# The first two attention tiles' values computed beside the last chunk of the first layer

## The chip, the cores and the metric

The kernel runs on one core of a Trainium2 chip. The metric is the device time of one execution in microseconds (us), shown as the median of several runs; lower is better. Beside these runs there is one profiled execution, from which every duration in this text is taken.

## The reference, cut to what matters

The input x is (4, 384, 64, 64) in float32, in other words 4 images of 384 channels and 4096 tokens. Two layers follow each other, each with a group norm ahead and a residual around it.

```python
x = x + L0(_gn(x), ...)   # a Mamba block over the 4096 tokens of each image
x = x + L1(_gn(x), ...)   # outlook attention, 3x3 windows at stride 2, 12 heads

# L0, after in_proj, causal convolution and silu:
def step(h, inp):
    dt_t, B_t, C_t, x_t = inp
    dA = jnp.exp(dt_t[:, :, None] * A[None])
    dBx = (dt_t * x_t)[:, :, None] * B_t[:, None, :]
    h = dA * h + dBx
    return h, jnp.einsum('bdn,bn->bd', h, C_t)
y = (jnp.moveaxis(ys, 0, 1) + xc * D) * _silu(z)
out = jnp.einsum('bld,cd->blc', y, out_proj_w)

# L1:
pooled = x.reshape(B, C, h, S, w, S).mean(axis=(3, 5))
a = softmax((einsum('bchw,ac->bhwa', pooled, attn_w) + attn_b) * scale)  # 9x9 a head and pixel
v = jnp.einsum('blkc,koc->blko', patches, Wg)       # nine 384x384 matrices
o = jnp.einsum('bnlpq,bnlqd->bnlpd', a, v)          # then folded back (3x3, overlapping)
y = jnp.einsum('bchw,oc->bhwo', folded, proj_w) + proj_b
```

The group norm needs the statistics of a whole image, so the second layer can start on an image only when the first layer has ended with that image. Image 0 is ready long before image 3 ends the first layer.

## The kernel before, in words

**The first layer** (`mamba_layer`, line 80) cuts the 4 images into 68 chunks of 241 tokens. Of a chunk, a *front* (norm, input projection, convolution, `dt`) runs ahead, then twelve *units* are scanned (768 channels of 16 states; a unit is two scans), then an *end* projects the result (`e_project`, line 681) and stores it to `x1` in device memory (`e_store`, line 689). A loop over steps `s` (line 776) writes the order of all engines out by hand. In step `s` unit `s` is scanned (DVE, `s_scan`), unit `s+1` gets its inputs (DVE, `s_inputs2`) and decays (ACT, `s_decay`), POOL multiplies unit `s-1` by C (`s_outputs`, line 642) and prepares unit `s+2` (`s_inputs`, line 598), PE sums the pair up to unit `s-2` into `y` each second step (`s_sum`, line 647), DVE gates a pair by `y` a step later (`s_gate`), and SP fetches units four steps ahead (`s_fetch`, line 585). Every engine executes its instructions in the order written: the class `InOrder` (line 34) puts all of them in program order, and since it issues them, the profile has them all under its line 45 and tells them apart by the names of the tiles.

The 68 chunks make 816 units. At `front_end`, step 803, the last front is done, the fronts' pools are closed (`fronts.close()`), and from there on each step ends with one call of `behind` (line 823), which is where work of the second layer is handed in. Matmul results of fronts and ends go through the PSUM pool `pmm`, two buffers in turn.

In the kernel before, `behind` steps through `outlook_weights` (line 1103), which loads the weights of the second layer: `wa` (attention weights, three DMAs), `wv` (the nine value matrices, three DMAs), then `ab`, `wpr`, `pb` and `own`, one DMA a step.

**The second layer** (`outlook_layer`, line 827) cuts the 4 images into 32 tiles of 8 rows, each 128 output pixels. A tile goes through these functions:

- `p_load` (887): 9 rows of `x1` to `xr` by DMA
- `p_pixels` (898): six ACT instructions apply the norm and sort the pixels into `xp` by window column; POOL clears the border; three DVE adds make the pooled pixels `t2`
- `p_weights` (932): 12 matmul records `psa`, then a chain on DVE and ACT to the softmax `at`, stored to `ads` in device memory
- `p_values` (957): for each of nine window positions three matmuls (six records) `psv`, an ACT copy to `vst`, and a DMA of three positions to `vds` in device memory
- `p_fetch_weights`, `p_fetch_values` (979, 982): both come back from device memory in another arrangement (`ain`, `vin`)
- `p_blocks` (985): block-diagonal weights `bd`, on ACT for rows 0 and 2, on POOL for rows 1 and 3
- `p_attend`, `p_fold` (1002, 1018): attention of one of four row pairs on PE into one PSUM buffer `ps`, added into `fold` by DVE
- `p_project` (1034): output projection `pso`, residual, store

The loop at line 1072 works on three tiles at once: `new` (i+2) is loaded and gets its pixels, `mid` (i+1) its weights and values, `old` (i) is attended. It begins at i = -2, when only tile 0 as `new` exists. `ads` and `vds` have two buffers each, with nine rows of zeros at their ends, written once at the start of the layer.

Of the kernel before, what the change touches and what calls it, by code (L numbers as in the profile page):

```python
# [12 lines left out]
P = 128  # L13
# [66 lines left out]
def mamba_layer(ctx, tc, x, w, x1, sc1, bi1, consts, behind):  # L80
# [695 lines left out]
    for s in range(-4, NU * (len(chunks) + 2)):  # L776
        k, m = divmod(s, NU)
        if m % 2 == 0 and unit(s + 4) is not None:
            s_fetch(s + 4)
        parts(s, EARLY)  # L780
        if m % 4 == 3 or s >= NU * len(chunks):
            norm_part(False)

        if (u := unit(s + 1)) is not None:
            s_inputs2(u)
        if (u := unit(s - 3)) is not None and not u.first:
            s_gate(u)
        parts(s, READY)

        b, ci = chunks[k][:2] if 0 <= k < len(chunks) else (B, 0)  # L790
        if b + 1 < B:
            n, e = divmod(NU * ci + m - 3, NU // 2)
            if e == 0 and 0 < n <= NCB * NX:
                x_stat(b + 1, n - 1, pending.pop())
            if e == 1 and 0 <= n < NCB * NX:
                pending.append(x_load(b + 1, n))
            if e == 2 and n == NCB * NX:
                x_coeffs(b + 1)
        for i in range(2):
            if (u := unit(s)) is not None:  # L800
                s_scan(u, i)
            if i == 1:
                parts(s, SCAN)
            if (u := unit(s + 1)) is not None:
                if i == 0:
                    s_carry(u)
                s_decay(u, i)
            if i == 0 and (u := unit(s - 1)) is not None:
                s_save(u)
        if (u := unit(s - 1)) is not None:  # L810
            s_outputs(u)
        norm_part(True)
        parts(s, POOL)
        if (u := unit(s + 2)) is not None:
            s_inputs(u)
        if (u := unit(s - 2)) is not None and not u.first:
            s_sum(unit(s - 3), u)
        parts(s, MID)
        parts(s, LATE)
        if s == front_end:  # L820
            fronts.close()
        if s >= front_end:
            behind()


@with_exitstack
def outlook_layer(ctx, tc, x1, w, out, sc1, bi1, consts, weights):

    nc = tc.nc
    B, _, H, W = out.shape
    NR = 4
    NW = W // 2
    NT = H // (2 * NR)
    ROWS = 2 * NR + 1  # L840
    HO = HEADS * KK
    NA = HO * KK
    NH = NA // 2
    NGW = 3
    VQ = 3
    scale = float(HD) ** -0.5
    pe, ve, ae, gp, sp = (
        InOrder(tc, e) for e in (nc.tensor, nc.vector, nc.scalar, nc.gpsimd, nc.sync)
    )

    wp = ctx.enter_context(tc.tile_pool(name="zero1", bufs=1))
    wa, ab, wv, wpr, pb, own = (weights[name] for name in ("wa", "ab", "wv", "wpr", "pb", "own"))

    ve.tensor_scalar_mul(wa, wa, 0.25)
    io = ctx.enter_context(tc.tile_pool(name="io1", bufs=3))
    act = ctx.enter_context(tc.tile_pool(name="act1", bufs=2))
    dram = ctx.enter_context(tc.tile_pool(name="dscr1", bufs=1, space=bass.MemoryType.DRAM))
    pa = ctx.enter_context(tc.tile_pool(name="pa", bufs=1, space=bass.MemoryType.PSUM))
    pv = ctx.enter_context(tc.tile_pool(name="pv", bufs=3, space=bass.MemoryType.PSUM))
    pt = ctx.enter_context(tc.tile_pool(name="pt", bufs=1, space=bass.MemoryType.PSUM))  # L860


    zero = wp.tile([KK, C], F32, tag="zero", name="zero")
    ve.memset(zero, 0.0)
    vds, ads = [], []
    for i in range(2):
        vd = dram.tile([P * KK + KK, C], F32, tag=f"vd{i}", name=f"vd{i}")
        ad = dram.tile([P * KK + KK, HO], F32, tag=f"ad{i}", name=f"ad{i}")
        sp.dma_start(vd[P * KK :, :], zero)
        sp.dma_start(ad[P * KK :, :], zero[:, :HO])  # L870
        vds.append(vd)
        ads.append(ad)

    class Tile:
        pass

    tiles = []
    for i in range(B * NT):
        c = Tile()
        c.i = i  # L880
        c.b, c.t = divmod(i, NT)
        c.first, c.last = c.t == 0, c.t == NT - 1
        c.lo = 1 if c.first else 0
        c.vin, c.ain, c.bd = {}, {}, {}
        tiles.append(c)

    def p_load(c):

        c.xr = io.tile([P, NCB, ROWS, W], F32, tag="xr", name="xr")
        for cb in range(NCB):  # L890
            sp.dma_start(
                c.xr[:, cb, c.lo :, :],
                x1[c.b, :, (2 * NR * c.t + c.lo - 1) * W : (2 * NR * c.t + ROWS - 1) * W].rearrange(
                    "(p cb) (r w) -> p cb r w", cb=NCB, w=W
                )[:, cb],
            )

    def p_pixels(c):


        b = c.b
        xp = act.tile([P, 3, NCB, ROWS, NW], F32, tag="xp", name="xp")
        gp.memset(xp[:, 0, :, :, 0:1], 0.0)
        if c.first:
            gp.memset(xp[:, :, :, 0, :], 0.0)
        for kj in range(3):
            j0 = 1 if kj == 0 else 0
            w0 = 2 * j0 + kj - 1
            for odd in range(2):
                r0 = 1 if odd else 2 * c.lo  # L910
                i0 = NR + 1 if odd else c.lo
                i1 = ROWS if odd else NR + 1
                ae.activation(
                    xp[:, kj, :, i0:i1, j0:],
                    c.xr[:, :, r0:ROWS:2, w0 : W - 2 + kj : 2],
                    AF.Identity,
                    bias=bi1[:, b : b + 1],
                    scale=sc1[:, b : b + 1],
                )
        c.xf = xp.rearrange("p kj cb r w -> p kj cb (r w)")  # L920
        c.t2 = act.tile([P, NCB, NR * NW], F32, tag="t2", name="t2")
        t3 = act.tile([P, NCB, NR * NW], F32, tag="t3", name="t3", bufs=1)
        ve.tensor_add(c.t2, pixel(c, 4), pixel(c, 5))
        ve.tensor_add(t3, pixel(c, 7), pixel(c, 8))
        ve.tensor_add(c.t2, c.t2, t3)

    def pixel(c, q):
        ki, kj = divmod(q, 3)
        row = (0, NR + 1, 1)[ki]
        return c.xf[:, kj, :, row * NW : (row + NR) * NW]  # L930

    def p_weights(c):

# [23 lines left out]
    def p_values(c, q):  # L957

        if q % VQ == 0:
            c.vst = act.tile([P, VQ, C], F32, tag="vst", name="vst", bufs=3)  # L960
        pix = pixel(c, q)
        psv = pv.tile([P, 512], F32, tag="pv", name="psv")
        for cb in range(NCB):
            pe.matmul(psv[:, :C], pix[:, cb, :], wv[:, cb, q, :], start=(cb == 0), stop=(cb == NCB - 1))
        ae.copy(c.vst[:, q % VQ, :], psv[:, :C])
        if q % VQ == VQ - 1:
            sp.dma_start(
# [101 lines left out]

        return (old, r) if r < NR else (mid, r - NR)  # L1070

    for i in range(-2, len(tiles) + 1):
        new, mid, old = tile_at(i + 2), tile_at(i + 1), tile_at(i)
        for r in range(NR):
            if old and r == 0:
                p_fetch_values(old, 0)
            if old and r + 1 < NR:
                p_fetch_values(old, r + 1)
            if mid and r == 0:
                p_weights(mid)  # L1080
            c, k = ahead(old, mid, r + 2)
            if c:
# [3 lines left out]
            for n, q in enumerate(qs):  # L1086
                if c:
                    p_blocks(c, k, n, len(qs))
                if mid:
                    p_values(mid, q)  # L1090
            if r == 0:
                if done := tile_at(i - 1):
                    p_project(done)
                if new:
                    p_load(new)
            if old:
                p_attend(old, r)
                p_fold(old, r)
            if r == 2 and new:
                p_pixels(new)  # L1100


def outlook_weights(ctx, tc, w, weights):

    wp = ctx.enter_context(tc.tile_pool(name="wp1", bufs=1, side="right"))
    sp = InOrder(tc, tc.nc.sync)
    na = HEADS * KK * KK
    shapes = {
        "wa": [P, NCB, na],
        "ab": [P, na],  # L1110
        "wv": [P, NCB, KK, C],
        "wpr": [P, NCB, NCB, P],
        "pb": [P, NCB],
        "own": [GW * KK, GW],
    }
    for name, shape in shapes.items():
        weights[name] = wp.tile(shape, F32, tag=name, name=name)
    for name in ("wa", "wv"):
        for cb in range(NCB):
            sp.dma_start(weights[name][:, cb], w[name][:, cb])  # L1120
            yield
    for name in ("ab", "wpr", "pb", "own"):
        sp.dma_start(weights[name], w[name])
        yield


@with_exitstack
def layers(ctx, tc, w, out):
# [14 lines left out]
    sc1 = cp.tile([P, B], F32, tag="sc1", name="sc1")  # L1143
    bi1 = cp.tile([P, B], F32, tag="bi1", name="bi1")
    consts = (blk12, ident, eps, one)
    weights = {}
    later = outlook_weights(ctx, tc, w, weights)
    mamba_layer(
        tc, x.rearrange("b c h w -> b c (h w)"), w, x1, sc1, bi1, consts, lambda: next(later, None)
    )  # L1150
    for _ in later:
        pass
    outlook_layer(tc, x1, w, out, sc1, bi1, consts, weights)


def layouts(inputs):
# [63 lines left out]
```

## Time and profile before

| | us |
|---|---|
| time, median of 3 runs (6319.99 to 6328.01) | 6324.49 |
| time of the profiled execution | 6322.35 |
| span of its trace, first to last instruction | 6320.6 |
| busy in it: PE / DVE / ACT / POOL | 5612.9 / 5377.6 / 4986.4 / 5311.3 |
| first fetch of a second-layer weight (`wa`, on SP) | at 4963.25 |
| last product on POOL in the first layer | ends 5037.64 |
| norm of the last image, last matmul | ends 5056.28 |
| `psa` of tiles 0, 1 and 2 | start 5070.77, 5104.21, 5140.01 |

The profile has busy times of the engines, their course in 40 slices of the span (158 us each), windows of any length, groups of instructions, and timelines for one engine: start, length, engine, operation, written tile <- read tiles, how many are merged in the line, and in brackets the idle time ahead and who ended it. PE is the matmul engine, PEld its weight loads, DVE the vector engine, ACT the scalar engine, POOL GpSimd, SP the engine that issues the DMAs.

### The profile page before, as it was taken

How to read it: one execution, taken by the hardware profiler on the slowest of the kernel's cores; microseconds unless marked ns; L12 is line 12 of the kernel's file. 1: busy time of each engine (PE TensorE's matmuls, PEld its weight loads, DVE VectorE, ACT ScalarE, POOL GpSimd, SP SyncE). 2: the span in 40 equal slices, each digit the busy share in tenths (PEclk: the TensorE clock that was granted, in tenths of full speed). 3: DMA queues.
4: the chain of work that ended last, by engine and by line, in shares of the span. 5: the costliest groups of instructions: out<-in, count | busy, mean ns of one | idle time of the engine just before them, and what ended most of it. 6: DMA issues, size and time to landing. Idle time of an engine off the chain costs nothing. (4 is left out here: it accounts for less than half of the span.)

```text
span 6320.6 us, 113305 instructions
## 1 busy us (share of the span) xinstructions
PE 5612.9 (89%) x40488; PEld 3956.3 (63%) x40488; DVE 5377.6 (85%) x4785; ACT 4986.4 (79%) x11842; POOL 5311.3 (84%) x2046
## 2 busy tenths in 40 slices
PE   6888888898888888888888888988898689999999
PEld 5666666666666666666666666666666345555555
DVE  4999999999999999999999999999999844554444
ACT  3888898888998889888898888889888644444453
POOL 3999999999999999999999999999999824333333
PEclk9899999999999999999998999999999799999999
DMA  4556555555555555555555555545555444445544
GB/s 127 132 134 149 147 131 140 126 139 147 134 142 139 139 139 134 131 142 137 147 145 131 135 128 138 139 127 135 130 133 138 137 138 164 166 165 171 170 165 143
DMA packets 635514, 893.42 MB, mean 141 GB/s; under 512 B 129913, under 2 KB 529067, under 8 KB 634436
## 3 DMA queue, kind: packets, MB, share of 16 engines
q1 hardware_dynamic: 634948, 886.17, 52.2%
q8 instruction: 319, 5.23, 0.4%
q14 instruction: 247, 2.02, 0.1%
HBM read 660.11 MB, written 225.70 MB: 140 GB/s over the span
## 5 line engine op out<-in xcount | busy, mean ns | idle before, releaser
L45 DVE TENSOR_TENSOR_SCAN h<-da,h 128x968 f32<-128x968 f32 x1632 | 3449.0, 2154 | 76.5 <-issue 51.8
L45 ACT ACTIVATE da<-dtr,aneg 128x241 f32<-128x241 f32 x6528 | 3036.6, 465 | 303.1 <-DVE h L45 137.8
L45 POOL TENSOR_TENSOR h<-h,bc 128x1928 f32<-128x1928 f32 x816 | 3228.9, 3957 | 12.8 <-DVE h L45 10.6
L45 POOL TENSOR_TENSOR h<-dxr,bc 128x964 f32<-128x964 f32 x816 | 1626.2, 1993 | 106.6 <-PE y L45 88.6
L45 PE MATMUL ps_in<-u,win 128*128 128x241 f32 x4896 | 1081.5, 374 | 85.8 <-DVE dtx L45 78.0
L45 PEld LDWEIGHTS ps_in<-u,win 128*128 128x128 f32 x4896 | 913.0, 191 | 252.1 <-DVE dtx L45 102.4
L45 POOL TENSOR_TENSOR bd<-ain,own 99x1188 f32<-99x1188 f32 x192 | 413.1, 2180 | 772.4 <-DMA ain<-ad 608.4
L45 DVE TENSOR_TENSOR h<-dxr,bp 128x964 f32<-128x964 f32 x816 | 928.1, 1137 | 105.2 <-PE y L45 88.9
L45 PE MATMUL y<-h,ssum 128*32 128x241 f32 x13056 | 909.0, 406 | 36.6 <-POOL h L45 35.4
L45 PEld LDWEIGHTS y<-h,ssum 128*32 128x32 f32 x13056 | 433.5, 119 | 455.0 <-issue 210.9
L45 PE MATMUL ps_cv<-xb,cdiag 128*128 128x241 f32 x3264 | 694.3, 368 | 6.0 <-ACT neg L45 4.5
L45 PEld LDWEIGHTS ps_cv<-xb,cdiag 128*128 128x128 f32 x3264 | 611.0, 189 | 79.3 <-issue 13.5
L45 PE MATMUL psv<-wv,xp 128*128 128x384 f32 x1728 | 587.9, 492 | 0.8 <-ACT vst L45 0.8
L45 PE MATMUL ps_xd<-xc,wx 128*56 128x241 f32 x816 | 300.5, 548 | 322.0 <-ACT xc L45 322.0
L45 ACT ACTIVATE bd<-ain,own 99x324 f32<-99x324 f32 x704 | 334.6, 555 | 293.0 <-PE ps L45 293.0
L45 PE MATMUL ps_out<-zs,wout 128*128 128x241 f32 (+1 forms) x2448 | 538.6, 369 | 0.0
L45 DVE TENSOR_TENSOR fold<-fold,ps 128x192 f32<-128x192 f32 (+1 forms) x768 | 211.1, 303 | 339.5 <-PE ps L45 326.3
L45 PEld LDWEIGHTS ps_out<-zs,wout 128*128 128x128 f32 x2448 | 471.1, 192 | 37.2
L45 PEld LDWEIGHTS psv<-wv,xp 128*128 128x128 f32 x1728 | 320.5, 190 | 224.3 <-issue 7.6
L45 PEld LDWEIGHTS ps_xd<-xc,wx 128*56 128x56 f32 x816 | 152.0, 195 | 460.7 <-ACT xc L45 347.5
L45 PE MATMUL ps_dt<-xd,wdt 25*128 25x241 f32 x816 | 252.7, 436 | 119.5 <-ACT dt L45 81.4
L45 PE MATMUL y<-xc,ddiag 128*128 128x241 f32 x816 | 277.2, 424 | 10.3 <-DVE zs L45 10.3
(105 smaller groups left out, 5355.9 us busy)
## 6 DMA issues: line engine op xcount, KB each, us to landing
dxr<-dxd SPq DMA_DIRECT2D x1632, 120.5 KB
dtr<-dtd SPq DMA_DIRECT2D x1632, 120.5 KB
bc<-bcd SPq DMA_DIRECT2D x544, 120.5 KB
vin<-vd SPq DMA_DIRECT2D x384, 148.5 KB
vd<-vst SPq DMA_DIRECT2D x96, 576.0 KB
dxd<-dtx SPq DMA_DIRECT2D x272, 180.8 KB
dtd<-dt SPq DMA_DIRECT2D x272, 180.8 KB
xs<-in_x SPq DMA_DIRECT2D x96, 256.0 KB
```

Source lines behind the costliest of these rows:

```text
L45: return self.tc.keep_in_program_order(issue(*args, **kwargs))
```

## The change

The nine value positions of tiles 0 and 1 are computed while the first layer's last chunk is scanned. `outlook_weights` is replaced by `outlook_before`, a generator that `behind` steps through from step 803 on, as before. It takes the room of the closed fronts and does the following, with a pause (`yield`) for each step:

1. load tile 0's rows and `wv`, now by window position in nine DMAs; make tile 0's pixels, two ACT instructions a step
2. tile 0's nine values, two positions a step, each with its own buffer `v` and its own DMA to `vds`; the load of tile 1's rows stands between the first and the second
3. tile 0's pooled pixels (three DVE adds), and the DMAs of the zero rows
4. the same for tile 1: pixels in three steps, values, pooled pixels, zero rows
5. close the pool `early` and load `wa`, `ab`, `wpr`, `pb` and `own` in its place, one DMA each, in one step

The values use the PSUM pool `pmm`, which the loop passes to `behind`. The second layer starts with the loads and attention weights of both tiles one after the other, then enters its loop at i = -1, and leaves out load, pixels, weights and values of the two tiles (`ready`) there. `zero` is cleared by POOL instead of DVE. The functions of a tile become methods of `OutlookTile`, with the same instructions.

```diff
         if s >= front_end:
-            behind()
+            behind(lambda: pmm.tile([P, 2, TM], F32, tag="mm", name="psv").rearrange("p a b -> p (a b)"))
...
+    def pixels(self, gp, ae, xp, sc1, bi1):
...
         gp.memset(xp[:, 0, :, :, 0:1], 0.0)
         if c.first:
             gp.memset(xp[:, :, :, 0, :], 0.0)
...
+            yield
...
+    def pool(self, ve, t2, t3):
+        self.t2 = t2
+        ve.tensor_add(t2, self.pixel(4), self.pixel(5))
+        ve.tensor_add(t3, self.pixel(7), self.pixel(8))
+        ve.tensor_add(t2, t2, t3)
+
+    def values(self, pe, wv, q, ps):
+
+        pix = self.pixel(q)
+        for cb in range(NCB):
+            pe.matmul(ps, pix[:, cb, :], wv[:, cb, q, :], start=(cb == 0), stop=(cb == NCB - 1))
...
-    for i in range(-2, len(tiles) + 1):
+    for c in ready:
+        p_load(c)
+        p_weights(c)
+    for i in range(-1, len(tiles) + 1):
...
-                if mid:
+                if mid and mid not in ready:
                     p_values(mid, q)
...
-            if r == 2 and new:
+            if r == 2 and new and new not in ready:
                 p_pixels(new)
...
+def outlook_before(ctx, tc, w, x1, H, W, sc1, bi1, dram, weights, ready):
...
+    with tc.tile_pool(name="before", bufs=1, side="right") as early:
+
+        zero = early.tile([KK, C], F32, tag="zero", name="zero")
+        gp.memset(zero, 0.0)
...
+        def load(i):
+            ready.append(OutlookTile(i, H, W))
+            ready[i].load(sp, x1, early.tile([P, NCB, ROWS, W], F32, tag="xr", name="xr"))
+
+        def pixels(i):
+            return ready[i].pixels(gp, ae, early.tile([P, 3, NCB, ROWS, NW], F32, tag="xp", name="xp"), sc1, bi1)
+
+        def value(i, q):
+            ps = psum()
+            ready[i].values(pe, wv, q, ps[:, :C])
+            v = early.tile([P, C], F32, tag="v", name="v", bufs=4)
+            ae.copy(v, ps[:, :C])
+            sp.dma_start(vds[i][: P * KK, :].rearrange("(p q) c -> p q c", q=KK)[:, q, :], v)
+
+        load(0)
+        made = pixels(0)
+        for q in range(KK):
+            sp.dma_start(wv[:, :, q, :], w["wv"][:, :, q, :])
+            if q % 2:
+                psum = yield
+                next(made, None)
+        for i in range(2):
+            if i == 1:
+                for _ in pixels(1):
+                    psum = yield
+            for q in range(KK):
+                value(i, q)
+                if q == 0 and i == 0:
+                    load(1)
+                if q % 2:
+                    psum = yield
+            ready[i].pool(ve, t2s[i], early.tile([P, NCB, NR * NW], F32, tag="t3", name="t3"))
+            sp.dma_start(vds[i][P * KK :, :], zero)
+            sp.dma_start(ads[i][P * KK :, :], zero[:, :HO])
+            psum = yield
     wp = ctx.enter_context(tc.tile_pool(name="wp1", bufs=1, side="right"))
...
     for name, shape in shapes.items():
         weights[name] = wp.tile(shape, F32, tag=name, name=name)
-    for name in ("wa", "wv"):
-        for cb in range(NCB):
-            sp.dma_start(weights[name][:, cb], w[name][:, cb])
-            yield
-    for name in ("ab", "wpr", "pb", "own"):
         sp.dma_start(weights[name], w[name])
-        yield
```

More of the change, by code (lines that the diff above doesn't have):

```diff
@@ L822, in mamba_layer @@
         if s >= front_end:
-            behind()
[L826 to L889, printed above, removed]
@@ new lines, in mamba_layer, with __init__, load @@
+            behind(lambda: pmm.tile([P, 2, TM], F32, tag="mm", name="psv").rearrange("p a b -> p (a b)"))
+NR = 4
+ROWS = 2 * NR + 1
+class OutlookTile:
+    def __init__(self, i, H, W):
+        self.NW = W // 2
+        NT = H // (2 * NR)
+        self.i, self.W = i, W
+        self.b, self.t = divmod(i, NT)
+        self.first, self.last = self.t == 0, self.t == NT - 1
+        self.lo = 1 if self.first else 0
+        self.vin, self.ain, self.bd = {}, {}, {}
+    def load(self, sp, x1, xr):
+        c, W = self, self.W
@@ L890, in p_load @@
         for cb in range(NCB):
             sp.dma_start(
-                c.xr[:, cb, c.lo :, :],
+                xr[:, cb, c.lo :, :],
                 x1[c.b, :, (2 * NR * c.t + c.lo - 1) * W : (2 * NR * c.t + ROWS - 1) * W].rearrange(
@@ L896, in p_load @@
             )
-    def p_pixels(c):
-        b = c.b
-        xp = act.tile([P, 3, NCB, ROWS, NW], F32, tag="xp", name="xp")
+        self.xr = xr
+    def pixels(self, gp, ae, xp, sc1, bi1):
+        c, W, b = self, self.W, self.b
         gp.memset(xp[:, 0, :, :, 0:1], 0.0)
@@ L919, in p_pixels, with pixel @@
                 )
+            yield
         c.xf = xp.rearrange("p kj cb r w -> p kj cb (r w)")
[L921 to L927, printed above, removed]
+    def pixel(self, q):
         ki, kj = divmod(q, 3)
         row = (0, NR + 1, 1)[ki]
-        return c.xf[:, kj, :, row * NW : (row + NR) * NW]
+        return self.xf[:, kj, :, row * self.NW : (row + NR) * self.NW]
@@ new lines, in pool, with outlook_layer, p_load, p_pixels @@
+    def pool(self, ve, t2, t3):
[7 more added lines that the diff above has]
+            pe.matmul(ps, pix[:, cb, :], wv[:, cb, q, :], start=(cb == 0), stop=(cb == NCB - 1))
+@with_exitstack
+def outlook_layer(ctx, tc, x1, w, out, sc1, bi1, weights, ready):
+    nc = tc.nc
+    B, _, H, W = out.shape
+    NW = W // 2
+    NT = H // (2 * NR)
+    HO = HEADS * KK
+    NA = HO * KK
+    NH = NA // 2
+    NGW = 3
+    VQ = 3
+    scale = float(HD) ** -0.5
+    pe, ve, ae, gp, sp = (
+        InOrder(tc, e) for e in (nc.tensor, nc.vector, nc.scalar, nc.gpsimd, nc.sync)
+    )
+    wa, ab, wv, wpr, pb, own, vds, ads = (
+        weights[name] for name in ("wa", "ab", "wv", "wpr", "pb", "own", "vds", "ads")
+    )
+    ve.tensor_scalar_mul(wa, wa, 0.25)
+    io = ctx.enter_context(tc.tile_pool(name="io1", bufs=3))
+    act = ctx.enter_context(tc.tile_pool(name="act1", bufs=2))
+    pa = ctx.enter_context(tc.tile_pool(name="pa", bufs=1, space=bass.MemoryType.PSUM))
+    pv = ctx.enter_context(tc.tile_pool(name="pv", bufs=3, space=bass.MemoryType.PSUM))
+    pt = ctx.enter_context(tc.tile_pool(name="pt", bufs=1, space=bass.MemoryType.PSUM))
+    tiles = ready + [OutlookTile(i, H, W) for i in range(len(ready), B * NT)]
+    def p_load(c):
+        c.load(sp, x1, io.tile([P, NCB, ROWS, W], F32, tag="xr", name="xr"))
+    def p_pixels(c):
+        xp = act.tile([P, 3, NCB, ROWS, NW], F32, tag="xp", name="xp")
+        for _ in c.pixels(gp, ae, xp, sc1, bi1):
+            pass
+        t2 = act.tile([P, NCB, NR * NW], F32, tag="t2", name="t2")
+        t3 = act.tile([P, NCB, NR * NW], F32, tag="t3", name="t3", bufs=1)
+        c.pool(ve, t2, t3)
@@ L960, in p_values @@
             c.vst = act.tile([P, VQ, C], F32, tag="vst", name="vst", bufs=3)
-        pix = pixel(c, q)
         psv = pv.tile([P, 512], F32, tag="pv", name="psv")
-        for cb in range(NCB):
-            pe.matmul(psv[:, :C], pix[:, cb, :], wv[:, cb, q, :], start=(cb == 0), stop=(cb == NCB - 1))
+        c.values(pe, wv, q, psv[:, :C])
         ae.copy(c.vst[:, q % VQ, :], psv[:, :C])
@@ L1078, in outlook_layer @@
                 p_fetch_values(old, r + 1)
-            if mid and r == 0:
+            if mid and r == 0 and mid not in ready:
                 p_weights(mid)
@@ L1093, in outlook_layer @@
                     p_project(done)
-                if new:
+                if new and new not in ready:
                     p_load(new)
@@ L1098, in outlook_layer @@
                 p_fold(old, r)
-            if r == 2 and new:
+            if r == 2 and new and new not in ready:
                 p_pixels(new)
-def outlook_weights(ctx, tc, w, weights):
+def outlook_before(ctx, tc, w, x1, H, W, sc1, bi1, dram, weights, ready):
+    nc = tc.nc
+    pe, ve, ae, gp, sp = (
+        InOrder(tc, e) for e in (nc.tensor, nc.vector, nc.scalar, nc.gpsimd, nc.sync)
+    )
+    NW = W // 2
+    HO = HEADS * KK
+    wp = ctx.enter_context(tc.tile_pool(name="wv1", bufs=1, side="right"))
+    wv = weights["wv"] = wp.tile([P, NCB, KK, C], F32, tag="wv", name="wv")
+    t2s = [wp.tile([P, NCB, NR * NW], F32, tag=f"t2{i}", name=f"t2{i}") for i in range(2)]
+    with tc.tile_pool(name="before", bufs=1, side="right") as early:
+        zero = early.tile([KK, C], F32, tag="zero", name="zero")
+        gp.memset(zero, 0.0)
+        vds = weights["vds"] = [dram.tile([P * KK + KK, C], F32, tag=f"vd{i}", name=f"vd{i}") for i in range(2)]
+        ads = weights["ads"] = [dram.tile([P * KK + KK, HO], F32, tag=f"ad{i}", name=f"ad{i}") for i in range(2)]
+        def load(i):
[30 more added lines that the diff above has]
+            psum = yield
@@ L1105, in outlook_weights @@
     wp = ctx.enter_context(tc.tile_pool(name="wp1", bufs=1, side="right"))
-    sp = InOrder(tc, tc.nc.sync)
-    na = HEADS * KK * KK
+    na = HO * KK
     shapes = {
@@ L1110, in outlook_weights @@
         "ab": [P, na],
-        "wv": [P, NCB, KK, C],
         "wpr": [P, NCB, NCB, P],
@@ L1117, in outlook_weights @@
         weights[name] = wp.tile(shape, F32, tag=name, name=name)
-    for name in ("wa", "wv"):
-        for cb in range(NCB):
-            sp.dma_start(weights[name][:, cb], w[name][:, cb])
-            yield
-    for name in ("ab", "wpr", "pb", "own"):
         sp.dma_start(weights[name], w[name])
-        yield
 @with_exitstack
@@ L1145, in layers, with behind @@
     consts = (blk12, ident, eps, one)
[L1146 to L1153, printed above, removed]
+    weights, ready = {}, []
+    later = outlook_before(ctx, tc, w, x1, H, W, sc1, bi1, dram, weights, ready)
+    def behind(psum):
+        try:
+            later.send(psum if started else None)
+        except StopIteration:
+            pass
+        started.append(True)
+    started = []
+    mamba_layer(tc, x.rearrange("b c h w -> b c (h w)"), w, x1, sc1, bi1, consts, behind)
+    outlook_layer(tc, x1, w, out, sc1, bi1, weights, ready)
 def layouts(inputs):
```

## The prediction

> **What bounds the kernel now.** I read the page's slices first, for the regimes; then the windows, for who is full in each; then the timeline of each engine across the border of the layers, 4935 to 5190 us, because everything that the change moves lies there.
>
> ```profile
> PE   6888888898888888888888888988898689999999
> DVE  4999999999999999999999999999999844554444
> POOL 3999999999999999999999999999999824333333
> ```
> There are two regimes. In the first layer POOL and DVE are full; in the second (from about slice 33) PE alone is.
>
> ```profile
> 4700.00:4800.00 100.00, 88.55 (x570) 64.95 (x566) 95.15 (x72) 86.95 (x215) 97.75 (x36) 0.90 0.52 131
> 4975.00:5000.00 25.00, 14.52 (x90) 8.62 (x91) 24.94 (x21) 18.00 (x47) 25.00 (x9) 0.73 0.89 279
> 5200.00:5300.00 100.00, 99.85 (x1016) 58.15 (x1015) 47.81 (x96) 52.04 (x106) 43.84 (x27) 1.00 0.49 162
> ```
> The columns are length, then busy time of PE, weight load, DVE, ACT and POOL, then clock, DMA share and GB/s. The middle line is the last chunk: without fronts, PE has 10 of 25 us free and ACT 7, POOL none. There is room on the engines that the values need, but POOL still sets the step (3.94 + 1.98 us, less overlap: 5.83).
>
> ```profile
> 5014.29 3.94 POOL L45 TENSOR_TENSOR h<-h,bc 128x1928 f32<-128x1928 f32 x1
> ...
> 5025.94 11.70 POOL L45 TENSOR_TENSOR h<-h,bc 128x1928 f32<-128x1928 f32 x3
> ```
> The first is unit 811's product. Its scan ended at 5008.37, so DVE runs 5.9 us ahead of POOL: the slack that anything added ahead of the scans may eat. POOL is gapless to 5037.64; behind it y and the last output projections end the layer.
>
> ```profile
> 4983.29 3.43 PE L45 MATMUL y<-h,ssum 128*32 128x241 f32 x28 [5.21 <-POOL h L45]
> ...
> 5037.69 3.43 PE L45 MATMUL y<-h,ssum 128*32 128x241 f32 x28 [2.89 <-POOL h L45]
> ...
> 5054.86 1.42 PE L45 MATMUL pv<-dev,blk 128*128 128x1 f32 x6
> 5070.77 6.55 PE L45 MATMUL psa<-wa,t 128*128 128x486 f32 x12 [14.49 <-issue]
> 5077.15 17.90 PE L45 MATMUL psv<-wv,xp 128*128 128x384 f32 x54
> 5104.21 6.89 PE L45 MATMUL psa<-wa,t 128*128 128x486 f32 x12 [9.16 <-DVE t L45]
> ```
> From the end of the last norm (5056.28) to tile 2's psa (5140.01, after which PE is gapless) pass 83.7 us: 14.5 us wait for tile 0's pixels, 9.2 for tile 1's, and two tiles' values (17.9 us each) are in it. This is what can be gained from.
>
> **What the Trainium skill says.** (1) "SBUF — State Buffer", section "Who interferes with whom": a DVE instruction with two SBUF inputs contends with a GpSimd instruction that reads SBUF, and whoever is first holds the port for its whole instruction. The trace agrees: the pooling adds take 0.56 us with POOL idle (5070.11), but beside POOL's three `bd` products (5096.54 to 5103.65) these, each ending as one product ends:
>
> ```profile
> 5098.61 3.00 DVE L45 TENSOR_TENSOR t<-xp 128x384 f32<-128x384 f32 x2 [11.82 <-ACT xp L45]
> 5101.65 2.41 DVE L45 TENSOR_TENSOR t<-t,t 128x384 f32<-128x384 f32 x1
> ```
> (2) "TensorE: Matmul & The Clock Gate", section "What's actually happening": after an idle stretch the array runs at half rate until it has been busy for some 3.4 us. The trace agrees: the 28 y matmuls take 3.43 us after a wait, 1.82 (at 5006.63) after dense projections.
>
> **The change part by part.** I use the clock of the trace before. The calls fall in steps 803 to 820: weights and tile 0's pixels in 803 to 807, its values two a step in 807 to 810 and the ninth, with the pooling adds, in 811; tile 1's pixels in 812 to 815, its values in 815 to 819; the other weights in 820.
>
> *Loads.* Steps 803 to 806 issue 0.8 MB of x1, 4.7 MB of wv and two fetches of 0.96 MB. At the 265 GB/s of 4965 to 4980 that is 28 us; the fetch of unit 810 lands near 4988, needed at 4995. The next fetch (812) stands on SP behind two value stores and tile 1's load, and lands near 5007 to 5010, needed at 5006.5: 0 to 3 us of POOL stall, which the wait below swallows. I take 0.
>
> *Tile 0's pixels.* Six ACT instructions (3.82 us), two a step, into idle gaps of 1.37 us a step: 0. POOL gets a memset of 9x384 (0.4 us, from 1.58 for 1782 elements) and two on xp (0.14 and 0.34): 0.9 us on the full engine.
>
> *Tile 0's values.* Two cost PE 4.1 us (4.14 for 12 matmuls). PE from the end of y at 4986.7: two values 90.8, projection 2.9 to 93.7, values 97.8, y 2.9 to 5000.7, values 04.8, two projections 10.6, values 14.7, y 17.6, the ninth 19.6. The copies (0.47 each on ACT) are hidden, but ACT is in order: unit 811's decays stand behind the copy of the first of those two projections (5007.7), so its scan starts at 5010.2, not 5004.1, and ends at 5014.5. POOL wants it at 5015.2: the slack is just spent, cost 0. With PE slower, each us costs one.
>
> *Tile 0's pooling.* Three adds with two SBUF inputs stand on DVE right behind scan 811, with POOL full. No row shows this pair; bounds are 1.7 us (three of 0.56) and the ends of three POOL instructions. I take the upper: the adds slip in at 5015.6, 5019.9 and 5022.3, the third when tile 1's first memset, which waits for xp, idles POOL. Then inputs 1.1, gate 0.4, scan 812 from 23.8 to 28.0. POOL takes it at 28.1 instead of 5020.1. Three units at DVE's pace (5.5 us) and the last product bring POOL's end to 5047.5: **+9.9 us** (with the lower bound 5040.1: +2.5).
>
> *Tile 1's values.* They stand in PE's queue before the last y and the projections of chunk 67. y of 812/813 ends at 41.2, four values 49.5, the last y 52.4 (not 5041.1), five values 62.6, three projections 8.6: 71.2, the last copy at **71.6 against 5051.2: +20.4** (+15 with the lower bound: PE's queue then limits). Pixels (4.1 us) find ACT idle; its adds find POOL idle.
>
> *Other weights.* wa waits for `early` to be free: v's last store at 63.2, the zero stores done near 65.7, then 1.5 MB: about 73. The norm ends at 71.6 + 5.1 = 76.7, then scaling (1.67 us): psa of tile 0 at 78.6. wa is hidden by 4 us; later than 76.8, each us costs one.
>
> *The start of the second layer.* psa 6.55: 85.1. Chain on DVE and ACT from psa's end to the store 9.5 (5077.33 to 5086.87): 94.6. psa of tile 1 runs beside it; its chain is queued on DVE: 104.1. Both tiles' rows are loaded a second time, three issues of 0.43 us each on an SP that waits anyway: 0. `ain` is issued only behind that second store on SP: 104.5, three issues and 2.3 us: 107.9. Eleven `bd` on ACT 5.2: 113.1. Tile 0's rows then come at the pace of bd, not PE: row 1 on POOL from 109.3, 6.44 + the fold memset 1.58: 117.3, fold 1.75, row 1's matmuls end at 120.9; row 2 at 124.6; row 3's bd waits for row 1's buffer: 127.5, matmuls to 129.3. psa of tile 2 at **5129.3 against 5140.0**.
>
> *Sum.* Norm's end to psa of tile 2: 129.3 - 76.7 = 52.6 instead of 83.7, -31.1; before it +20.4. **-10.7 us.** The profiled execution took 6322.35 (span 6320.6): 6311.6. The median shown is 2.1 above it: 6313.8, said as 6313.
>
> **The rivals.** *Faster:* the adds slip between POOL's instructions (+2.5) and the last y comes earlier: +15.0 instead of +20.4, so -16, and to -25 if tile 0's rows follow at PE's pace (four of 1.75 us = 7) instead of the 16.2 from 113.1 to 129.3. For it: the adds are short and POOL's queue has gaps. Against: the two fenced rows. 6299 to 6308.
>
> *Slower:* the half clock. At 4965 to 4970 the granted clock is 0.50. If the values run so, each costs 4.0 instead of 2.0, and y and projections cost 1.6 and 2 more. Nine values in steps 807 to 811 bring up to 18 us past a slack that is spent, and nine at the end 18 in series: up to +36, to 6350. It decides where more than 10.7 us come together, some six values at half clock. For it: PE waits for POOL each second step. Against: projections behind a y already run at 2.61 us for 12, full rate, and the queue above has no gap of 3 us.
>
> *No gain:* wa or a fetch lands 10 us later than worked out, as SP's queue holds them behind stores that wait for ACT. -2 to +8; 6322 to 6332. Against: both have 4 us or a later wait to hide in.
>
> **How the numbers follow.** Forecast -10.7 (own range -18 to -3): 0.48. Faster: 0.26. Slower: 0.14. No gain: 0.12. About 0.2% (12.6 us) is what a measurement of this kernel can tell from no change. My forecast lies just inside: a third of its chance (0.17) is beyond, with the faster rival 0.43; slower takes 0.14; the rest, 0.43, is within. Range: -27 to +5 from 6324.5, 6297 to 6330: below lies little of the faster rival, above most of the slower one and a part of no gain, under 0.2 in all.
>
> **What would show it.** DVE's adds t<-xp near 5014: 2 us and more each confirm the lock. POOL's gap before unit 812's product: about 8 us, none under the faster rival. PE gapless from 4986 to 5020 at clock 1.0; 0.5 there is the slow rival. Output projections of chunk 67 ending near 5071, psa at 5079, psa of tile 2 near 5129. I am wrong if the tail grows by over 31 us, or if tile 0's rows take 37 us as before.

## The result, and the profile after

The changed kernel takes 6318.18 us in the median of 12 runs (6304.38 to 6326.56), the kernel before 6326.01 us in the median of 12 (6318.14 to 6329.44). The ratio is 0.9988, with a 95% interval of 0.9979 to 0.9997: between 2 and 13 us are gained. The profiled execution has a span of 6316.6 us.

The page's slices of the changed kernel:

```profile
PE   6888888898888888888888898988988779999999
DVE  4999999999999999999999999999999844544444
POOL 3999999999999999999999999999999924333333
```

At this width almost nothing moves: PE rises in slice 32, where the values have gone, and falls by a step in the slice behind it. The windows show the last chunk (same columns as before; the stretch is 5.6 us later, as explained below):

```profile
4980.60:5005.60 25.00, 18.47 (x98) 10.39 (x98) 21.30 (x18) 18.50 (x47) 25.00 (x9) 0.74 0.90 279
```

PE is busy for 18.5 of 25 us instead of 14.5. DVE falls from 24.9 to 21.3: it has lost its lead and waits. POOL is still full here.

To compare the executions I count all times from the start of the last `bp` matmul of the first layer (the last chunk's `f_b`, in step 802, the last front work ahead of the change): 4954.47 us before, 4960.07 after. The 5.6 us between them arise in the part of the program that the change leaves alone; they are the spread of single executions (in all eight traces of this document it lies between 4953.56 and 4967.80).

| from the last `bp` | before | after | difference |
|---|---|---|---|
| last product on POOL ends | 83.2 | 88.0 | +4.8 |
| last norm matmul ends | 101.8 | 118.0 | +16.2 |
| psa of tile 0 starts | 116.3 | 120.2 | +3.9 |
| first attention matmul starts | 162.4 | 155.9 | -6.5 |
| psa of tile 2 starts | 185.5 | 174.7 | -10.8 |
| end of the span | 1366.1 | 1356.5 | -9.6 |

The tail of the first layer grows by 16 us, the start of the second gives 27 back. The timeline of PE in the changed kernel answers to the one shown of before:

```profile
4989.91 3.42 PE L45 MATMUL y<-h,ssum 128*32 128x241 f32 x28 [4.80 <-POOL h L45]
4993.27 4.33 PE L45 MATMUL psv<-wv,xp 128*128 128x384 f32 x12
...
5020.64 1.84 PE L45 MATMUL y<-h,ssum 128*32 128x241 f32 x32
...
5054.36 9.94 PE L45 MATMUL psv<-wv,xp 128*128 128x384 f32 x30
...
5080.23 7.92 PE L45 MATMUL psa<-wa,t 128*128 128x486 f32 x12 [2.19 <-issue]
5089.57 5.16 PE L45 MATMUL psa<-wa,t 128*128 128x486 f32 x12 [1.42 <-DVE at L45]
5115.99 3.11 PE L45 MATMUL ps<-bd,vin 99*32 99x99 f32 x72 [21.26 <-ACT bd L45]
```

The first value starts the instant the y of its step is done, and PE then has no gap until the y of units 808 and 809 at 5020.64, which has all its 32 products at once: POOL had long delivered them. Ten more us of values (the line at 5054.36) stand ahead of the last output projections. In the second layer the two psa now follow each other, and then PE idles 21 us for the first `bd`.

What the late y does is in POOL's timeline:

```profile
5015.14 3.93 POOL L45 TENSOR_TENSOR h<-h,bc 128x1928 f32<-128x1928 f32 x1
5022.64 1.98 POOL L45 TENSOR_TENSOR h<-dxr,bc 128x964 f32<-128x964 f32 x1 [3.58 <-PE y L45]
5024.58 3.93 POOL L45 TENSOR_TENSOR h<-h,bc 128x1928 f32<-128x1928 f32 x1
```

The idle time is in the brackets: POOL wants to prepare unit 813 and waits 3.58 us for PE's y. The pool of `h` has five buffers, so unit 813 takes the one of unit 808, which that y is still to read. Before the change that y had ended at 5008.45, and the same preparation followed POOL's product without a wait:

```profile
5012.35 1.99 POOL L45 TENSOR_TENSOR h<-dxr,bc 128x964 f32<-128x964 f32 x1
```

In this gap of the changed kernel, on DVE, lie tile 0's pooling adds:

```profile
5015.86 4.24 DVE L45 TENSOR_TENSOR_SCAN h<-da,h 128x968 f32<-128x968 f32 x2 [2.17 <-POOL h L45]
5020.02 1.00 DVE L45 TENSOR_TENSOR t<-xp 128x384 f32<-128x384 f32 x2
5021.05 0.56 DVE L45 TENSOR_TENSOR t<-t,t 128x384 f32<-128x384 f32 x1
```

They take 1.56 us together, the price with POOL idle. The chain of waits of the changed kernel says the same from the end (start, length, what):

```profile
5006.50 4.07 PE psv L45 x12
5010.57 5.70 PE ps_out L45 x28
5016.27 4.03 PE psv L45 x12
5020.30 2.19 PE y L45 x34
```

Here PE itself is the path: two values, two output projections, two values, and only then the y.

### The profile page after: what moved, and what is told of

It reads as the page before. It is cut to its first block, busy times and chain, and to the rows that moved or that the text cites. A ratio compares the mean times of both kernels' runs of the same rounds, so it can differ in the third digit from the quotient of the medians.

```text
span 6316.6 us, 113361 instructions
## 1 busy us (share of the span) xinstructions
PE 5629.0 (89%) x40488; PEld 3968.2 (63%) x40488; DVE 5369.9 (85%) x4784; ACT 4986.2 (79%) x11842; POOL 5311.1 (84%) x2047
## 4 chain that ended last, share of the span: by engine, by line
PE 23%; ACT 17%; DVE 11%; issue 3%; DMA 1%; POOL 1%; SPq 1%; ACTq 0%; DVEq 0%; POOLq 0%
ACT da L45 10%; DVE h L45 8%; PE psv L45 6%; PE pso L45 4%; PE ps L45 4%; PE psa L45 3%; PE y L45 2%; PE ps_in L45 1%; ACT xc L45 1%; DVE at L45 1%; PE ps_xd L45 1%; DVE mx L45 1%; ACT L45 1%; POOL h L45 1%; ACT dt L45 1%
## 6 DMA issues: line engine op xcount, KB each, us to landing
vin<-vd SPq DMA_DIRECT2D x384, 148.5 KB
```

## The experiments

In all texts of expectations the marks are counted from the last `bp`, as above. The first four runs were compared with 62 runs of the kernel before (median 6325.91 us), the last two with 9 (6325.95 us). The marks that each left (the ratio is worked out from all runs and is not the quotient of the two medians):

| | POOL ends | norm ends | psa of tile 2 | median us | ratio to before, 95% |
|---|---|---|---|---|---|
| changed kernel | 88.0 | 118.0 | 174.7 | 6318.18 | 0.9988 (0.9979 to 0.9997) |
| x1_noadds | 87.6 | 117.6 | 174.5 | 6314.77 | 0.9982 (0.9975 to 0.9990) |
| x2_thin | 94.0 | 122.9 | 178.6 | 6320.36 | 0.9988 (0.9981 to 0.9994) |
| x3_one_tile | 88.1 | 106.4 | 176.0 | 6314.2 | 0.9985 (0.9979 to 0.9992) |
| x4_start | 87.9 | 117.9 | 171.0 | 6311.25 | 0.9978 (0.9968 to 0.9989) |
| x6_gap | 87.7 | 104.1 | 159.0 | 6299.68 | 0.9958 (0.9945 to 0.9970) |
| x7_gap_thin | 84.3 | 99.7 | 152.3 | 6296.27 | 0.9957 (0.9943 to 0.9972) |

### x1_noadds: the pooling adds taken away

```diff
-            ready[i].pool(ve, t2s[i], early.tile([P, NCB, NR * NW], F32, tag="t3", name="t3"))
+            if i == 0:
+                ready[0].t2 = t2s[0]
+                ae.copy(t2s[0], ready[0].pixel(4))
+            else:
+                ready[i].pool(ve, t2s[i], early.tile([P, NCB, NR * NW], F32, tag="t3", name="t3"))
```

> Tile 0's three pooling adds on DVE are left out: ACT copies one of the four pixels into t2 instead, so tile 0 is not pooled. Marks are counted from the start of the last chunk's bp matmul (before: POOL's last product ends at +83.2, last norm matmul at +101.8, psa of tile 2 at +185.5; changed kernel: +88.0, +118.0, +174.7). Theory A (the adds ran in a gap that POOL had anyway, because the h buffers are held by a y that PE does late): nothing moves by more than 1 us, POOL's gap of 3.6 us stays, POOL ends at +87 to +89. Rival B (the adds on DVE are what the tail pays): POOL ends 2 to 8 us earlier, +80 to +86, and the gap shrinks.

POOL ends at 87.6, the norm at 117.6, and the gap is there as in the changed kernel, in the timeline of POOL:

```profile
5017.84 1.97 POOL L45 TENSOR_TENSOR h<-dxr,bc 128x964 f32<-128x964 f32 x1 [3.47 <-PE y L45]
```

So the adds cost at most 0.4 us in the changed kernel, and the 3.5 us are not theirs: theory A. The interval of the whole time overlaps that of the changed kernel.

### x2_thin: the y no longer late

```diff
-            for q in range(KK):
-                value(i, q)
...
+            plan = (((0, 1), (2,), (3, 4), (), (5, 6), (7, 8)), ((0, 1), (2, 3, 4), (5, 6, 7), (8,)))[i]
+            for qs in plan:
+                for q in qs:
+                    value(i, q)
...
+                if qs is not plan[-1]:
+                    psum = yield
```

> Tile 0's values are spread over steps 807 to 812 as 2, 1, 2, 0, 2, 2 instead of 2, 2, 2, 2, 1, with no value in the step that has two output projections; tile 1's follow one step later. Theory A (the late y holds the h buffers): POOL's gap of 3.6 us goes or falls under 1 us, and the adds, now in step 812, meet a POOL at work: 2 us and more each, 5 us or more for the three, against 1.6 in the changed kernel; POOL ends between +84 and +88. Rival B (y is not the cause): the gap stays within 1 us of 3.6 and POOL ends at +88 or later. Whole time within 5 us of the changed kernel under both.

POOL no longer waits for a y anywhere. But the adds, now one step later, meet a POOL that works. First DVE, then POOL, from the timeline of this run:

```profile
5034.28 7.85 DVE L45 TENSOR_TENSOR t<-xp 128x384 f32<-128x384 f32 x2
5042.17 0.56 DVE L45 TENSOR_TENSOR t<-t,t 128x384 f32<-128x384 f32 x1
```

```profile
5039.28 1.97 POOL L45 TENSOR_TENSOR h<-dxr,bc 128x964 f32<-128x964 f32 x1
5042.19 0.14 POOL L45 MEMSET xp<- 128x27 f32 x1 [0.94 <-DVE t L45]
5048.09 3.95 POOL L45 TENSOR_TENSOR h<-h,bc 128x1928 f32<-128x1928 f32 x1 [5.75 <-DVE h L45]
```

The first two adds take 7.85 us. The first alone lasts 7.38: it ends when POOL has run out of work at 5041.25 and stands at its memset of `xp`, which waits for these adds. The third is then free. Behind them the scan of the next unit is late, and POOL waits 5.75 us for it, then 1.56 and 0.31 for the two after it. POOL ends at 94.0, later than the 84 to 88 that I had expected: I was right that the gap goes and that the lock appears (the adds waiting for POOL's products), and had priced the lock too low. That the whole is no slower than the changed kernel (0.9988 both) is within the spread of the runs; the trace has psa of tile 2 3.8 us later.

### x3_one_tile: tile 1 back in the second layer

```diff
-        for i in range(2):
-            if i == 1:
-                for _ in pixels(1):
-                    psum = yield
+        for i in range(1):
...
-                if q == 0 and i == 0:
-                    load(1)
...
```

> Only tile 0 is made beside the first layer; tile 1 is loaded, normed and given its values in the second layer as before. Theory A (tile 1's values only stand in PE's queue ahead of the last projections, and what they save later is idle PE time): last norm matmul near +107 instead of +118, but psa of tile 2 near +173, so the whole is within 4 us of the changed kernel, 8 to 14 us faster than before. Rival C (each tile brings its half): psa of tile 2 near +180, the whole about 5 us faster than before.

The norm ends at 106.4 instead of 118.0, and psa of tile 2 starts at 176.0 instead of 174.7. That is between the two theories, 3 us later than A's 173 and 4 earlier than C's 180. The timeline of PE shows why no more is lost:

```profile
5063.11 7.40 PE L45 MATMUL psa<-wa,t 128*128 128x486 f32 x12 [2.19 <-issue]
5095.17 6.73 PE L45 MATMUL psa<-wa,t 128*128 128x486 f32 x12 [24.66 <-issue]
5101.74 5.97 PE L45 MATMUL psv<-wv,xp 128*128 128x384 f32 x18
```

Tile 1's pixels are late, PE waits 24.7 us for them, and then does tile 1's values beside tile 0's rows, where it would wait for `bd` otherwise. The second tile, as the change places it, pays 11.6 us in the first layer and gets 12.8 back in the second: 1.2 us in the traces for 18 us of matmuls moved. The whole is 4 us below the changed kernel in the medians, with overlapping intervals.

### x4_start: tile 0's fetches ahead of tile 1's weights

```diff
-    for c in ready:
-        p_load(c)
-        p_weights(c)
+    p_weights(ready[0])
+    for r in range(2):
+        p_fetch_weights(ready[0], r)
+        p_fetch_values(ready[0], r)
+    p_load(ready[0])
+    p_weights(ready[1])
+    p_load(ready[1])
...
```

> The changed kernel with tile 0's first two fetches of weights and values issued right behind its own store, ahead of tile 1's attention weights, and the rows loaded after. Theory A (the start of the second layer is a chain through tile 1's softmax, which tile 0's first fetch waits for on SP): bd of row 0 starts behind tile 1's exp, 7 to 8 us earlier, psa of tile 2 at +166 to +168, the whole 7 us faster than the changed kernel and 15 to 19 faster than before. Rival D (bd and the fold memset set the pace of tile 0's rows anyway, or the tail does): under 3 us.

This lies between the two. The first attention matmul starts 7.4 us earlier (at 148.5), as theory A has it, but psa of tile 2 only 3.7 us earlier. The timeline of PE has the starts of rows 1 and 2:

```profile
5110.64 3.11 PE L45 MATMUL ps<-bd,vin 99*32 99x99 f32 x72 [5.46 <-DVE fold L45]
5116.36 3.11 PE L45 MATMUL ps<-bd,vin 99*32 99x99 f32 x72 [2.61 <-ACT bd L45]
```

Row 1 waits 5.46 us for row 0's fold instead of 2.32, since the fold waits for POOL's memset of `fold`, which stands behind POOL's own `bd` and ends at 5108.60. This is rival D's wait, and it takes 3.1 of the 7.4 us. Row 2 waits for its `bd`, which waits for its own fetch; that still stands on SP behind tile 1's store and the second load of the rows. The timeline of ACT:

```profile
5111.19 5.12 ACT L45 ACTIVATE bd<-ain,own 99x324 f32<-99x324 f32 x11 [9.16 <-DMA ain<-ad]
```

The two waits run side by side and end almost together: with `bd` in time, row 2 would start only some 0.55 us earlier (2.61 us of wait instead of the 2.06 behind a fold), and with the memset in time it would still wait for `bd`. In the medians the kernel is 6.9 us below the changed one, with overlapping intervals.

### x6_gap and x7_gap_thin: tile 1's values into the gap of the second layer

If PE idles 21 us behind psa of tile 1, and tile 1's 18 us of values stand in its way in the first layer, they belong into that gap. Both kernels keep tile 0 and tile 1's pixels beside the first layer (`xp` moves to the pool of `wv`, so that it lives on), and contain x4_start. Tile 1's pooling moves into the second layer too, and with tile 1's work gone `wa` is loaded in step 815 of x6_gap.

```diff
+    ready[1].pool(ve, t2, act.tile([P, NCB, NR * NW], F32, tag="t3", name="t3", bufs=1))
+    p_weights(ready[0])
...
+    p_values(ready[1], 0)
+    p_values(ready[1], 1)
+    p_weights(ready[1])
+    for q in range(2, 6):
+        p_values(ready[1], q)
...
+            if i == 0 and r > 0:
+                p_values(mid, 5 + r)
```

> As x4_start, and tile 1's values and pooling are moved into the second layer's first gap of PE, behind psa of tile 0 (two values), psa of tile 1 (four) and tile 0's rows (three); beside the first layer stay tile 0 whole and tile 1's pixels. Theory A (tile 1's values cost their full PE time ahead of the last projections, while PE idles 21 us behind psa of tile 1): POOL ends at +88 as in the changed kernel, last norm matmul near +107, psa of tile 2 at +156 to +161, the whole 22 to 30 us faster than before. Rival C (PE's idle time at the start is no room, since the copies on ACT and bd get into each other's way): psa of tile 2 at +167 or later, no gain over x4_start.

POOL ends at 87.7, psa of tile 2 starts at 159.0, and the median is 26 us below before: theory A in all three. The norm ends at 104.1, 3 us ahead of the 107 expected; no run takes that apart.

x7_gap_thin differs only in the steps: one value a step in 807 to 815, tile 0's adds in step 816, tile 1's pixels behind them.

```diff
         for q in range(KK):
             value(0, q)
             if q == 0:
                 load(1)
-            if q % 2:
-                psum = yield
+            psum = yield
```

> As x6_gap, with tile 0's values one a step over steps 807 to 815, its pooling adds in step 816, behind the last scan, and tile 1's pixels behind that. Theory A (late y costs 3.6 us through the h buffers, the adds nothing): POOL ends at +84 to +85, last norm matmul near +103, psa of tile 2 at +152 to +157, the whole 26 to 34 us faster than before, 3 to 4 faster than x6_gap. Rival B: POOL ends at +87 or later and the whole equals x6_gap.

POOL has no gap at all and ends at 84.3, 1.1 us later than before; the memsets ahead of its last products alone are 0.94. The norm ends at 99.7, ahead of the 103 expected and even ahead of the kernel before (101.8). In part this is PE's clock: at the last y, which a value stands ahead of here, the granted clock is 1.00 and the 28 matmuls take 1.83 us; in the kernel before it was 0.50 and they took 3.43. The adds stand beside POOL's last products and take 6.6 us there, but no scan is behind them any more. The timeline of PE at the start of the second layer:

```profile
5062.31 6.74 PE L45 MATMUL psa<-wa,t 128*128 128x486 f32 x12 [2.19 <-issue]
5068.88 4.03 PE L45 MATMUL psv<-wv,xp 128*128 128x384 f32 x12
5072.75 5.05 PE L45 MATMUL psa<-wa,t 128*128 128x486 f32 x12
5077.64 5.97 PE L45 MATMUL psv<-wv,xp 128*128 128x384 f32 x18
```

The values fill what was idle. The median is 6296.27 us, 29.7 below before; its lead over x6_gap is 6.7 us in the marks (psa of tile 2), 3.4 in the medians and 0.9 in the means of five runs each, so in the whole time it is not shown. Its median lies below that of both kernels, the one before and the changed one.

A sixth `h` buffer, the most direct test, was not tried; that the five buffers are what holds POOL is read from the code and from the wait, and x2 and x7 show only that it goes with the late y.

## Why the prediction was right, point by point

The forecast was -10.7 us. At psa of tile 2, the point up to which the sum was made, the traces show -10.8, and the runs -7.8 with an interval that includes it. The total fits better than its terms do: the tail of the first layer grew by 16.2 us where the sum had 20.4, and the start of the second gave back 27.0 where it had 31.1. These two errors of about 4 us cancel, and that they do is luck.

**Loads, pixels, copies at nothing: held.** No stall of POOL or ACT for tile 0's rows or weights. The memsets cost 0.41 + 0.53 us on POOL, as priced (0.9). The late fetch of unit 812, kept as 0 to 3 us of POOL stall, cost none in the changed kernel; in x4_start, same code at this place, the profile has 1.1 us for it, in x1_noadds 0.17.

**Tile 0's values on PE: held.** From the end of y to the end of the ninth value I had 32.9 us; it took 31.3 (4993.3 to 5024.6), without a gap, at full clock. The slow rival, values at half clock, is refuted there: two cost 4.1 us.

**"The slack is just spent, cost 0": failed.** I followed PE's delay through ACT to the scans and stopped there. The y that PE does late also holds `h` buffers, and POOL's next preparation writes into one of them. That wait was worked out nowhere, and costs 3.58 us. The numbers for it were there: in my own queue that y ends at 5017.6, and POOL's preparation of unit 813 stood at 5012.35 in the trace before; with 0.9 us of memsets this makes an estimate of 4.3 us. x1 shows that the wait doesn't depend on the adds, x2 and x7 that it goes when the values are thinned out.

**"I take the upper" for tile 0's pooling: failed, by its circumstances.** I priced the adds at 7.7 us beside a working POOL. They took 1.56, as POOL was idle just then, because of the very wait that I had missed. So the two signs that I had named for it, adds of 2 us and more each and a gap of about 8 us ahead of unit 812's product, did not show. The lock itself is real: x2 takes the wait away, and the same three adds then take 8.4 us, with POOL's end 6.0 us behind the changed kernel's and 9.7 behind that of x7, where no scan stands behind them. Counted from before, x2's POOL ends 10.8 us later, close to the +9.9 of my upper bound. The two mistakes belong together, one hides the other's cost: POOL's end moved +4.8, not +9.9.

**Tile 1's values ahead of the last projections: held.** From POOL's end to the norm's end there were 18.6 us before and 30.0 after, +11.4 where the sum had +10.5 (20.4 - 9.9). x3 gives the same from the other side: without tile 1's values the norm ends 11.6 us earlier.

**Other weights last: held.** `wa` is issued 10.4 us ahead of the norm's end (5067.64), and psa of tile 0 starts 2.19 us behind it. In x6, where `wa` is issued 22 us ahead, psa starts 2.2 us behind it too, so the late load costs nothing.

**The start of the second layer: 4 us short.** Up to the first row the chain is the one worked out (two softmax chains of 9.7 and 9.3 us, store, fetch, eleven `bd`). From the norm's end to psa of tile 2 it took 56.8 us, not 52.6. Two terms were too small, and both are PE's own. psa of tile 0 took 7.92 us instead of 6.55, at a granted clock of 0.64 instead of 0.78; in the seven traces where it starts 2.2 us behind the norm it takes 6.7 to 8.2, so this term differs from execution to execution. And from the end of the first `bd` to psa of tile 2 I had 16.2 us, where it took 18.9: each row took 3.11 us instead of 1.75, at a granted clock of 0.50 instead of 1.00, behind a PE that had idled for 21 us. The first row of the kernel before, with the values around it, reads

```profile
5110.94 5.97 PE L45 MATMUL psv<-wv,xp 128*128 128x384 f32 x18
5116.84 1.75 PE L45 MATMUL ps<-bd,vin 99*32 99x99 f32 x72
5118.52 4.14 PE L45 MATMUL psv<-wv,xp 128*128 128x384 f32 x12
```

and that of the changed kernel stands above, at 5115.99. So the rows came not at the pace of `bd`, as I had it, but of PE and the fold in turn: rows 1 to 3 start 2.06 to 2.32 us behind the end of the row before, when its fold is done (at row 2 a fetch of `vin` lands in the same moment), and their `bd` had ended 0.65 us earlier or more. Before, and in x3, tile 1's values stand between the rows, and a row that runs in one piece takes 1.75 to 1.77 us; in the four traces without them (changed kernel, x1, x2, x4) all take 3.11. I had cited the half clock ("TensorE: Matmul & The Clock Gate", "What's actually happening") as a danger in the tail, where PE turned out dense, and not asked for it in the start, where the change had just made PE sparse.

**The rivals.** *Faster* (the adds slip in, -16 or more) had the adds right, but not what opened the gap for them. *Slower* and *no gain* did not happen.

## What to carry to other kernels

Moving work from a full engine's stage into another stage's idle time paid here only what the receiving queue had free at that place: 18 us of tile 1's matmuls brought 1.2 us in the traces ahead of the last projections; put into idle time of their own layer, with the fetches in a better order, the kernel gained 18.5 us more (x6_gap). When a queue is made later, follow each buffer that its instructions read back to whoever writes it next, not only the results that they deliver. And an instruction's price beside a full engine may change with the very delay that the change brings: look where it falls, before taking a bound.

## What had not been expected of the hardware

The Trainium skill ("SBUF — State Buffer", "Who interferes with whom") has the shared port held for one whole instruction. In the second layer before the change, that is what two-input adds on DVE waited for: about one `bd` product each (three products of 2.4 us; 3.00 us for the first two adds, 2.41 for the third). Beside POOL's products of the first layer, the first add waited through several of them: 7.38 us in x2, until POOL's queue stood still, and 5.56 us in x7, until the last of three products had ended. So the end of the running instruction is no bound for the wait. In both places POOL's products followed each other without a gap that the profile shows; what decides who gets the port next, no run here separates.
